# How the reciprocals of the softmax sums reach HBM in turned order: a DMA of single numbers, or a TensorE transpose

## The chip, the cores and the metric

The kernel runs on one core of one Trainium2 chip. The metric is the device time of one execution in microseconds (us); the kernel before took 951.88 us, the median of three runs (951.11 to 956.85). A profile of one execution goes with it. Its engines are PE (TensorE matmuls), PEld (TensorE weight loads), DVE (VectorE), ACT (ScalarE), POOL (GpSimd) and SP (SyncE, which here only issues DMAs). A `q` behind an engine's name means its instruction queue: `SPq` and `ACTq` rows are DMAs being issued.

## What is computed

The reference is one transformer block with adaptive layer norm: 4 batches of 512 tokens with 256 features, 16 attention heads, and a mixture of 16 experts behind the attention. The change touches the attention alone:

```
scores = (einsum('bhqd,bhkd->bhqk', q, k) + einsum('bhqd,bhkd->bhqk', q_rope, k_rope)) * scale
attn = softmax(scores, axis=-1)
out = einsum('bhqk,bhkd->bhqd', attn, v)
out = out.transpose(0, 2, 1, 3).reshape(b, s, H * HD) @ Wout
```

## The kernel before

**Pairs and slots.** The attention goes through 32 head pairs (4 batches of 8 pairs, line 913), numbered `g` from 0 to 31; `LASTP` is 31. A pair has 8 slots: 2 heads by 4 tiles of 128 queries. In a slot, TensorE forms a 128 x 512 tile of scores (`score`, L732) in PSUM. VectorE takes each row's negated maximum (L740), ScalarE computes the exponentials and, in the same instruction, their row sums (L748, into one column of `den[g]`). VectorE transposes the exponentials in blocks of 32 x 32 into `a` (L759). The exponentials are not divided by their sums here; the division comes later, on the small result.

**Turning the blocks.** A full transpose needs the blocks moved between partitions as well. After the last slot, `move(g)` (L768) takes the reciprocals `rd` of the sums (128 queries by 8 numbers, L771) and issues 16 DMAs of 128 KB each from `a` to `et` (L779), 32 rows of 4 KB in each. They are called a train below. `et` has one buffer. `values(g)` (L816) multiplies `et` with the compressed keys and values into `cx` (L823, 16 matmuls), at the start of the pair after the next.

**The division.** `cx` has queries along its free dimension, so its division needs the reciprocals along the free dimension too, repeated on 64 partitions for each head. `everywhere(g)` (L784) does that: TensorE transposes `rd` into a PSUM tile of 8 x 128 (L787), in the `st` ring of four tiles that the scores use as well; one slot later ScalarE copies it to SBUF (L792), and a DMA of 8 rows of 512 bytes writes it to `rdd` in HBM (L793). Two DMAs then read it back, each repeated over 64 partitions, into `rdb` (L795). VectorE multiplies `cx` by `rdb` into `ctxT` (L836), which `project` (L842) multiplies with the output weights.

**Order.** The order on TensorE, VectorE, ScalarE and SP is the order in which the program issues its instructions. The loop at L918 defers each slot's follow-up work to the next slot by the list `then_do`. So, for pair `g`, `move(g)` runs in slot 0 of pair `g+1`; the transpose of `rd` is issued at the end of slot 2 and the copy and the three DMAs follow in slot 3. Pair 31 divides its exponentials at once (L755, L756) and uses no `rdb`. For pair 30 (`LASTP - 1`) half of the train and the write to `rdd` go through ScalarE's queue instead of SP's.

**What else SP issues.** Weights of the experts (L478, L479) in the last batch at slot 4, rows of `xs` for the first expert tiles (L466) in slots 5 and 6 of two pairs, some broadcasts (L162), and register loads before the `xs` rows (L434). ScalarE issues a few: `h2d` (L228) and `tab` (L399), which carry the routing's results to HBM. DMAs of SP and ScalarE take eight completion semaphores (numbers 101 to 108 in the trace) in turn, and a DMA is issued only when the earlier DMA of its semaphore has landed.

After the attention, 79 expert tiles and the shared feed-forward part follow (from L1083), which the change does not touch.

Of the kernel before, what the change touches and what calls it, by code (L numbers as in the profile page):

```python
# [13 lines left out]
F32 = mybir.dt.float32  # L14
# [7 lines left out]
P = 128  # L22
B, S, D = 4, 512, 256
NT = S // P
# [45 lines left out]
def adaln_block(ctx: ExitStack, tc: tile.TileContext, a: dict):  # L70
    nc = tc.nc
# [4 lines left out]
    ident = const.tile([P, P], F32, name="ident")  # L76
# [22 lines left out]
    rdd = dram.tile([B * NPAIR, 2 * NT, P], F32, name="rdd")  # L99
# [3 lines left out]
    psum = ctx.enter_context(tc.tile_pool(name="psum", bufs=2, space=PSUM))  # L103
# [386 lines left out]
    with ExitStack() as actx:  # L490
        aw = actx.enter_context(tc.tile_pool(name="aw", bufs=1))
        big = actx.enter_context(tc.tile_pool(name="big", bufs=2))
        tmp = actx.enter_context(tc.tile_pool(name="tmp", bufs=2))
# [131 lines left out]
        st = {}  # L625
# [111 lines left out]
        def soft(g, slot, pc):  # L737

            nm = tmp.tile([P, 1], F32, tag="nm", name=f"nm_{g}_{slot}", bufs=4)
            nc.vector.tensor_reduce(nm, pc, AX.X, ALU.max, negate=True)  # L740
            if slot == 0:
                den[g] = tmp.tile([P, 2 * NT], F32, tag="den", name=f"den_{g}", bufs=2)
                at[g] = tmp.tile([P, NT, 2, NT, NT, 32], F32, tag="a", name=f"a_{g}")
            if g < LASTP:
                e = tmp.tile([P, S], F32, tag="e", name=f"e_{g}_{slot}", bufs=4)
            else:
                e = at[g].rearrange("p l s h t j -> p (l s h t j)")[:, ts(slot, S)]
            nc.scalar.activation(e, pc, AF.Exp, bias=nm, accum_out=den[g][:, slot : slot + 1])  # L748
            es[g, slot] = e

            def after():
                s, t = divmod(slot, NT)
                if g == LASTP:
                    rd = tmp.tile([P, 1], F32, tag="rd1", name=f"rd_{g}_{slot}", bufs=4)
                    nc.vector.reciprocal(rd, den[g][:, slot : slot + 1])  # L755
                    nc.vector.tensor_scalar(e, e, rd, None, ALU.mult)  # L756
                    return

                nc.vector.transpose(  # L759
                    at[g][:, :, s, :, t, :].rearrange("p l h j -> p h l j"),  # L760
                    e.rearrange("p (h l j) -> p h l j", l=NT, j=32),
                )
                if slot == 2 * NT - 1:
                    move(g)

            return after

        def move(g):  # L768

            rd = tmp.tile([P, 2 * NT], F32, tag="rd", name=f"rd_{g}", bufs=2)  # L770
            nc.vector.reciprocal(rd, den[g])  # L771
            rds[g] = rd

            et[g] = tmp.tile([P, NT, 2, NT, P], F32, tag="et", name=f"et_{g}", bufs=1)

            for q in range(NT):
                for l in range(NT):
                    queue = nc.scalar if g == LASTP - 1 and q >= NT // 2 else nc.sync
                    queue.dma_start(  # L779
                        et[g][ts(l, 32), q].rearrange("p s h n -> p (s h n)"),  # L780
                        at[g][ts(q, 32), l].rearrange("p s h t j -> p (s h t j)"),
                    )

        def everywhere(g):  # L784

            pr = psum.tile([2 * NT, P], F32, tag="st", bufs=4, name=f"prd_{g}")
            nc.tensor.transpose(pr, rds[g], ident)  # L787
            rdT = tmp.tile([2 * NT, P], F32, tag="rdT", name=f"rdT_{g}", bufs=1)
            rdb[g] = tmp.tile([P, S], F32, tag="rdb", name=f"rdb_{g}", bufs=1)

            def after():
                nc.scalar.copy(rdT, pr)  # L792
                (nc.scalar if g == LASTP - 1 else nc.sync).dma_start(rdd[g], rdT)  # L793
                for s in range(2):
                    nc.sync.dma_start(  # L795
                        rdb[g][ts(s, 64), :],
                        rdd[g, ts(s, NT), :].rearrange("t p -> (t p)").unsqueeze(0).to_broadcast([64, S]),
                    )

            return after  # L800

# [112 lines left out]
        LASTP = len(pairs) - 1  # L914
        den, at, es, et, rds, rdb = {}, {}, {}, {}, {}, {}
        then_do = []
        ahead = None
        for g, (b, j) in enumerate(pairs):  # L918
            then = pairs[g + 1] if g < LASTP else None
            for slot in range(2 * NT):  # L920
# [28 lines left out]
                if slot == 2 and g:  # L949
                    then_do.append(everywhere(g - 1))  # L950
# [132 lines left out]
    turned, chosen, g, yts = {}, {}, {}, {}  # L1083
# [131 lines left out]
```

## Time and profile before

| | |
|---|---|
| median of three runs | 951.88 us |
| the profiled execution | 950.73 us |
| its span, first to last instruction | 948.5 us |
| mean granted TensorE clock | 0.98 |
| the 32 head pairs, scores to last ctxT | about 33 to 653 us of the span |
| transposes of rd (L787) | 31 of 0.27 us |
| copies of the transposed rd (L792) | 31 of 0.24 us |
| writes of rdd issued (L793) | 30 by SP, 1 by ScalarE, median 0.42 us to issue |
| et DMAs issued (L779) | 488 by SP, median 0.59 us; 8 by ScalarE |
| DMA packets | 79,361, 140.64 MB |

A row of the timeline has the start in us from the span's start, the duration in us, engine, line, operation, the tiles written and read, and, where instructions in a row were merged, their count; a bracket tells for how long the engine stood idle before it and what ended that. A row of the waits has who waited, for what, the time in total, the number of times and the longest, in us. The stretches view gives, for each stretch of time, its length and the busy time of each engine with its number of instructions.

### The profile page before, as it was taken

The page shows a single profiled execution, that of the slowest core. Times are in us where ns is not written, and L with a number is a line of the kernel's source. Part 1 is how long each engine was busy: PE and PEld are TensorE (multiplying, and loading weights), DVE is VectorE, ACT ScalarE, POOL GpSimd, SP SyncE. Part 2 cuts the span into 40 slices and gives each one's busy share as a digit, 9 for nine tenths or more (in the row PEclk, how much of TensorE's full clock was granted, in tenths as well). Part 3 has the DMA queues.
Part 4 walks back from the last instruction along what each step waited for, and adds up shares of the span by engine and source line. Part 5 has one row for each costly group of instructions (what it writes and reads, how often), then busy time and mean ns, then how long its engine had stood idle before and what let it go on. Part 6 is the DMA issues. An engine that isn't in the chain of part 4 may idle for free. (4 is left out here: it accounts for less than half of the span.)

```text
span 948.5 us, 12482 instructions
## 1 busy us (share of the span) xinstructions
PE 884.5 (93%) x3199; PEld 476.6 (50%) x3199; DVE 630.2 (66%) x1377; ACT 429.3 (45%) x1030; POOL 451.9 (48%) x412
## 2 busy tenths in 40 slices
PE   5888999999999999998999998959899999999996
PEld 3323444444444444453444454425666677777754
DVE  1488688788879888879988889844353332232258
ACT  2344545464644654554455554423533434444410
POOL 3644355355634776843377864313624623433421
PEclk9899999999999999999999999979989999999999
DMA  9526466575456665555477776675553443333274
GB/s 253 184 68 145 113 143 151 125 161 127 100 134 156 164 176 142 128 132 139 107 182 181 210 178 171 173 195 182 182 139 90 136 133 96 112 119 95 66 282 161
DMA packets 79361, 140.64 MB, mean 148 GB/s; under 512 B 22873, under 2 KB 47160, under 8 KB 79292
## 3 DMA queue, kind: packets, MB, share of 16 engines
q1 hardware_dynamic: 71352, 119.84, 50.6%
q0 software_dynamic: 6864, 16.86, 4.9%
q10 hardware_dynamic: 1076, 3.15, 1.0%
q8 instruction: 27, 0.44, 0.2%
q14 instruction: 42, 0.34, 0.1%
HBM read 51.35 MB, written 25.39 MB: 81 GB/s over the span
## 5 line engine op out<-in xcount | busy, mean ns | idle before, releaser
L732 PE MATMUL psc<-w 128*128 128x512 f32 x512 | 264.2, 609 | 22.9 <-ACT a L748 11.5
L748 ACT ACTIVATE e<-psc,nm 128x512 f32<-128x512 f32 x248 | 170.3, 687 | 219.6 <-DVE nm L740 218.6
L740 DVE TENSOR_REDUCE nm<-psc 128x1 f32<-128x512 f32 x256 | 171.5, 670 | 68.0 <-PE psc L732 67.6
L711 POOL TENSOR_TENSOR w<-w 128x512 f32<-128x512 f32 x64 | 81.6, 1276 | 199.0 <-ACT w L708 196.9
L759 DVE STREAM_TRANSPOSE a<-e 128x512 f32<-128x512 f32 x248 | 172.0, 694 | 0.1
L1022 POOL DMA_INDIRECT ys<-y,xt x79 | 77.2, 977 | 138.4 <-ACT y L1021 125.7
L732 PEld LDWEIGHTS psc<-w 128*128 128x128 f32 x512 | 92.1, 192 | 95.1 <-issue 66.6
L823 PE MATMUL cx<-et,ckv 128*64 128x512 f32 x512 | 117.8, 602 | 3.5 <-DVE rows L183 1.2
L996 PE MATMUL ph<-w,xT 128*128 x316 | 108.7, 467 | 1.0 <-DVE xT L990 0.7
L714 POOL TENSOR_TENSOR w<-w 64x512 f32<-64x512 f32 x64 | 82.1, 1283 | 37.8 <-DVE w L713 34.0
L1002 DVE TENSOR_TENSOR g<-g,ph 128x176 f32<-128x176 f32 x79 | 26.7, 338 | 93.8 <-ACT g L1001 93.8
L1017 PE MATMUL py<-w,gT 88*128 x316 | 83.0, 385 | 3.2 <-ACT gT L1010 3.2
L715 POOL TENSOR_TENSOR w<-w 64x512 f32<-64x512 f32 x64 | 80.9, 1264 | 4.7
L858 PEld LDWEIGHTS po<-wvo,ctxT 128*128 128x128 f32 x256 | 48.4, 192 | 61.3 <-issue 59.0
L858 PE MATMUL po<-wvo,ctxT 128*128 128x256 f32 x256 | 76.7, 384 | 0.8 <-DVE ctxT L834 0.8
L823 PEld LDWEIGHTS cx<-et,ckv 128*64 128x64 f32 x512 | 35.1, 137 | 82.4 <-issue 59.2
L1017 PEld LDWEIGHTS py<-w,gT 88*128 88x128 f32 x316 | 60.5, 192 | 25.2 <-ACT gT L1010 5.2
L197 POOL DMA_INDIRECT xs<-rows,si x48 | 47.7, 994 | 42.0 <-ACT a L748 24.1
L996 PEld LDWEIGHTS ph<-w,xT 128*128 128x128 f32 x316 | 54.9, 194 | 18.9 <-issue 1.0
L705 PE MATMUL ppk<-w 128*128 128x512 f32 x128 | 63.0, 615 | 0.0
L705 PE MATMUL ppq<-w 128*128 128x512 f32 x128 | 61.0, 599 | 1.4 <-DVE ctxT L836 1.4
L1021 ACT ACTIVATE y<-py,xt 128x256 f32<-128x256 f32 x79 | 37.4, 473 | 46.0 <-PE py L1017 46.0
(201 smaller groups left out, 1107.1 us busy)
## 6 DMA issues: line engine op xcount, KB each, us to landing
et<-a SPq DMA_DIRECT2D x488, 128.0 KB
xt<-xs SPq DMA_DIRECT2D x79, 129.0 KB
w<-ys SPq DMA_DIRECT2D x16, 512.0 KB
rdb<-rdd SPq DMA_DIRECT2D x62, 128.0 KB
w<-in_we SPq DMA_DIRECT2D x16, 352.0 KB
w<-in_wl SPq DMA_DIRECT2D x16, 176.0 KB
xs<-fill SPq DMA_DIRECT2D x17, 129.0 KB
x<-in_x SPq DMA_DIRECT2D x4, 512.0 KB
```

The lines of the kernel that those rows point to most:

```text
L705: nc.tensor.matmul(pp, w_j[:, j, ts(k, P)], d["hT"][:, k, :], start=(k == 0), stop=(k == KD - 1))
L711: nc.gpsimd.tensor_tensor(t1, t0[which], rope[:, 0, :], ALU.mult)
L714: nc.gpsimd.tensor_tensor(dst[64:128, 0, :], t1[64:128, :], t3[which][64:128, :], ALU.add)
L715: nc.gpsimd.tensor_tensor(dst[0:64, 1, :], t1[0:64, :], t3[which][0:64, :], ALU.add)
L732: nc.tensor.matmul(pc, st[b]["qb"][j][:, s, ts(t, P)], kb[j % 2][:, s, :], start=True, stop=True)
L740: nc.vector.tensor_reduce(nm, pc, AX.X, ALU.max, negate=True)
L748: nc.scalar.activation(e, pc, AF.Exp, bias=nm, accum_out=den[g][:, slot : slot + 1])
L759: nc.vector.transpose(at[g][:, :, s, :, t, :].rearrange("p l h j -> p h l j"), e.rearrange("p (h l j) -> p h l j", l=NT, j=32),)
L823: nc.tensor.matmul(cx[s * 64 : s * 64 + 64, :].rearrange("p (q n) -> p q n", q=NT), d["ckv"][:, k, 0, :], et[g][:, :, s, k, :], start=(k = ...
L858: nc.tensor.matmul(d["po"][t2][:, t % 2, :], d["ctxT"][j][:, ts(t, P)], wvo[:, j, :], start=False, stop=(j == NPAIR - 1 and t % 2 == 1),)
L996: nc.tensor.matmul(ph, xT[:, k, :], we[:, k * 2 * I : (k + 1) * 2 * I], start=(k == 0), stop=(k == KD - 1),)
L1017: nc.tensor.matmul(py, gT[:, f, :], we[0:I2, WE + f * D : WE + (f + 1) * D], start=(f == 0), stop=(f == 1))
```

## The change

For pairs 0 to 29 the reciprocals are written to HBM straight from `rd`: one DMA on SP, issued in `move(g)` ahead of the train, with `rdd[g]` viewed as 128 x 8, so that each of the 1,024 numbers of 4 bytes goes to its own place. The transpose, its PSUM tile, ScalarE's copy and the DMA behind it are gone for these pairs. The two DMAs that read `rdd` back stay in slot 3. Pair 30 keeps the old way.

```
         def move(g):
             rd = tmp.tile([P, 2 * NT], F32, tag="rd", name=f"rd_{g}", bufs=2)
             nc.vector.reciprocal(rd, den[g])
             rds[g] = rd
+            if g < LASTP - 1:
+
+                nc.sync.dma_start(rdd[g].rearrange("t p -> p t"), rd)
...
         def everywhere(g):

-            pr = psum.tile([2 * NT, P], F32, tag="st", bufs=4, name=f"prd_{g}")
-            nc.tensor.transpose(pr, rds[g], ident)
-            rdT = tmp.tile([2 * NT, P], F32, tag="rdT", name=f"rdT_{g}", bufs=1)
             rdb[g] = tmp.tile([P, S], F32, tag="rdb", name=f"rdb_{g}", bufs=1)

-            def after():
-                nc.scalar.copy(rdT, pr)
-                (nc.scalar if g == LASTP - 1 else nc.sync).dma_start(rdd[g], rdT)
+            def spread_out():
                 for s in range(2):
                     nc.sync.dma_start(
                         rdb[g][ts(s, 64), :],
                         rdd[g, ts(s, NT), :].rearrange("t p -> (t p)").unsqueeze(0).to_broadcast([64, S]),
                     )
+
+            if g < LASTP - 1:
+                return spread_out
+            pr = psum.tile([2 * NT, P], F32, tag="st", bufs=4, name=f"prd_{g}")
+            nc.tensor.transpose(pr, rds[g], ident)
+            rdT = tmp.tile([2 * NT, P], F32, tag="rdT", name=f"rdT_{g}", bufs=1)
+
+            def after():
+                nc.scalar.copy(rdT, pr)
+                nc.scalar.dma_start(rdd[g], rdT)
+                spread_out()

             return after
```

## The prediction

> **What bounds the kernel now.** I read the page's busy shares first, then single head pairs in the stretches view, then TensorE's and SP's timelines, then SP's waits.
>
> ```profile
> PE 884.5 (93%) x3199; PEld 476.6 (50%) x3199; DVE 630.2 (66%) x1377; ACT 429.3 (45%) x1030; POOL 451.9 (48%) x412
> ```
>
> One head pair, from one start of the cx matmuls to the next (PE, PEld, DVE, ACT and POOL busy, then clock, DMA share and GB/s):
>
> ```profile
> 166.57:183.35 16.78, 16.78 (x52) 7.45 (x51) 13.09 (x25) 8.59 (x23) 8.73 (x8) 1.00 0.61 141
> 183.35:200.13 16.78, 16.78 (x52) 7.45 (x52) 14.04 (x32) 7.94 (x21) 8.58 (x7) 1.00 0.61 141
> ```
>
> TensorE is busy for all of the 16.78 us, at full clock, and VectorE has some 3 us left. TensorE sets the pace of such pairs. The transpose that goes stands in it so:
>
> ```profile
> 322.34 0.27 PE L787 MATMUL prd<-ident,rd 128*8 128x128 f32 x1
> 322.45 1.02 PE L732 MATMUL psc<-w 128*128 128x512 f32 x2
> ```
>
> It lasts 0.27 us, but the next matmul starts 0.11 us after it: ends are modelled and matmuls overlap, so 0.11 is what it takes of the pace.
>
> The second loop is the train of 16 DMAs that turns et:
>
> ```profile
> 318.05 10.06 SPq L779 DMA_DIRECT2D et<-a  x16
> 328.20 0.42 SPq L793 DMA_DIRECT2D rdd<-rdT  x1
> 330.31 1.12 SPq L795 DMA_DIRECT2D rdb<-rdd  x2
> ```
>
> et has one buffer: a train starts when the cx matmuls of the pair before have ended, takes SP 10.06 us to issue, and its data is read by the next cx matmuls at 331.14. From the timelines I took, for each of the 30 trains that the change touches, two margins. *Cover* is the time from the reciprocal's end to the train's start: mean 1.9 us, and none in trains 0, 12, 20, 22 and 25. *Slack* is the time from the landing (last packet plus 0.6 us, the gap where TensorE does wait) to the cx matmuls: mean 1.8 us, none in trains 0, 11, 13, 19 and 29. So TensorE waits for et in five trains and is close to it in others. SP's waits say the same of the cover:
>
> ```profile
> SPq L779 <- PE cx L823: 54.7, 24, 4.5
> SPq L795 <- DMA rdd<-rdT: 50.6, 31, 3.4
> ```
>
> **Removed.** *TensorE:* 30 transposes x 0.11 us = 3.3 us. Where TensorE waits for et (five trains) the time is given back at the wait, so 25 x 0.11 = **-2.7**; nothing if something else fills the pace. *ScalarE:* 30 copies x 0.24 us, nothing: ScalarE is 45% busy and waits for VectorE's maxima. *PSUM:* one of four st buffers is free for some 3 us more in each pair; TensorE's waits for an st buffer all stand seven or more score matmuls behind the transpose, where it is no longer among the last four tiles, so nothing. *SP's wait* of 50.6 us for rdd: rdb can follow the train at once, some 2.0 us sooner, because the numbers went out 10 us before. rdb's reader is a pair away, so that itself brings 0 (at most the 2.2 us that VectorE now waits for rdb). But what is queued behind rdb on SP moves too: expert weights and xt loads in the last batch. One place has them on the path:
>
> ```profile
> 616.66 0.54 SPq L478 DMA_DIRECT2D w<-in_we  x1
> ...
> 621.28 11.30 SPq L779 DMA_DIRECT2D et<-a  x8
> ```
>
> ```profile
> 619.09 12.57 ACTq L779 DMA_DIRECT2D et<-a  x8
> 631.70 0.69 ACT L748 ACTIVATE a<-psc,nm 128x512 f32<-128x512 f32 x1 [12.57 <-DMA et<-a]
> ```
>
> SP and ScalarE take the same eight DMA semaphores in turn, and a DMA waits until the earlier one of its semaphore has landed. Here the last train waits for weight loads so, ScalarE stands for 12.57 us, and TensorE for 11.55. Weights issued 1.9 us earlier (end of rdb at 616.56 against 614.65) should land that much earlier: **-1.9** (0 if transfers, not issues, set it).
>
> **Added.** A DMA of 128 x 8 single numbers on SP, ahead of the 16 et DMAs, waiting for the reciprocal. All 16 are queued behind it, and the cx matmuls wait for them. *Issue:* the row with as many pieces (128 x 8, of 512 bytes) is
>
> ```profile
> 3.80 1.38 SPq L534 DMA_DIRECT2D w<-in_wqr  x2
> ```
>
> 0.67 us each. The upper end is the value loads, also 1,024 pieces but behind full queues: 4.37 us for two, 2.2 each. I take 0.67, since the queues are nearly empty when it is issued (DMA share 0.09 from 330 to 332 us). *Transfer:* the nearest row writes 17 single numbers to HBM through one DMA engine; first its issue on ScalarE's queue, then the DMA queues in the 0.2 us after it (packets, MB, share of 16 engines; one packet is the semaphore's):
>
> ```profile
> 463.34 0.48 ACTq L399 DMA_DIRECT2D tab<-ei  x1
> ```
>
> ```profile
> q10 hardware_dynamic: 18, 0.00, 4.9%
> ```
>
> Its packets are 6 ns apart (464.06 to 464.17), and SP, which waits for it, goes on at 464.59. The new DMA has 64 numbers on each of 16 engines: 64 x 6 ns = 0.4 us, landing some 1.8 us after its issue. The Trainium skill speaks against this: "DMA: Bandwidth & Descriptors", Specifications, says that below 512 bytes the engine reads, modifies and writes, and its section "Latency and other measured facts" gives 0.2 us for an HBM access. One after another, 64 x 0.2 = 12.8 us an engine (estimate from that page). The row contradicts that for 17 numbers: they would take 3.4 us, and all took 1.25. I take the row. But another row makes me keep a wide upper end: the third tab, 46 numbers on two engines, has its last packet at 709.51 and is recorded as landed at 713.94, and packets of xt beside it took up to 3.7 us where 47 ns is usual. That is (713.94 - 709.51)/46 = 96 ns a number; nothing in the trace tells why this one was slow.
>
> Let X be the time by which the numbers hold up a train that has no cover. A train loses max(0, X - cover - slack), and the sum over the 30 trains is: X 0.75: 0.8 us (train 0 alone); 2.0: 4.8; 3.0: 13.5; 5.0: 49; 6.0: 73; 12.8: 273. A pair that is held up gives the next train more cover, so the loss is between half of that sum and all of it. With issue 0.67 + 0.05 and the transfer beside the train's spare DMA time (share 0.91), X = 0.75: **+0.8**. At 2.2 us of issue it is about +6.
>
> *Semaphores in turn:* each pair still issues 19 DMAs, but one of them moves ahead of the train. Five trains (11, 19, 21, 27, 29) stop because ScalarE's h2d or tab DMA has the semaphore that a late et DMA needs, for example
>
> ```profile
> SPq L779 <- DMA tab<-ei: 2.0, 1, 2.0
> ```
>
> If the stop comes one et DMA earlier, one more has to be issued behind it: 5 x 0.63 us, less 0.2 of slack = +3.0; if the stops fall away, the waits of trains 11, 19 and 29 go (1.2 + 0.5 + 0.4): -2.0. The order can't be read from the trace; I take **+1.5**, half of the case in which the stop moves.
>
> POOL's queue and ScalarE's order are not passed by anything that moves; rd has two buffers, so the reciprocal that would wait for the new DMA to read is two pairs away.
>
> **Sum.** -2.7 - 1.9 + 0.8 + 1.5 = -2.3 us. The profiled execution took 950.73 us (span 948.5 and 2.2 around it), so 948.4; the median of the runs is 1.15 above it: 951.88 - 2.3 = **949.6**. About 1% (9.5 us) is what a measurement of this kernel can tell from no change.
>
> **Rivals.**
>
> *A, likeliest, 53%: within 1%.* As summed. With TensorE's gain lost, the issue at 2.2 us and the semaphores at +3.0 it ends near 958; with all ends good, near 944. Its own range is 944 to 958.
>
> *B, 32%: slower, the small writes are slow to drain.* Place: the et trains. At 96 ns each, spread over the engines, 64 x 0.096 = 6.1 us; less the 1.0 us that a train's own first packet needs anyway and what spare DMA time regains, X is about 5.2: 27 to 54 us, say 40, which gives some 990. It decides from X of 2.9 to 3.7 us on, where the loss passes 11.8 us. For it: the third tab, and 16 numbers going to each 64-byte stretch of rdd. Against it: two of the three tabs. Also for it in part: the new DMA's semaphore is the one that the eighth et DMA takes, 4.5 us into the train.
>
> *C, 11%: the writes go through one place in HBM, one after another.* At 12.8 us of X: 1,090 to 1,220; at 1,024 x 96 ns = 98 us, half of 30 x (98 - 3.7), or more: over 2,300. Against it: scatters of 1,032-byte rows, whose ends are partial too, land in 2.4 us at best, as most scatters of whole rows do.
>
> *D, 4%: faster.* The turn of semaphores happens to spare the last train its waits: of TensorE's 11.55 us some 8 more go, 941.
>
> The range that leaves out C and most of D, with B up to X of about 6: 944 to 1003. Faster by over 1%: 0.04; within: 0.53; slower: 0.43.
>
> **What would show it.** The new DMA's row with 0.7 us (2.2 would be the upper end); its start at the reciprocal's end, and trains still starting as the cx matmuls end; trains still of 10.06 us (longer, with a stop at the eighth DMA, is B); no wait of SP for rdd; TensorE's wait near 620 us at 9 to 10 us. Pairs of 16.67 us confirm the 0.11. The forecast is wrong if TensorE waits for et in most pairs, or if the last train's stop changes by several us.

## The result, and the profile after

The changed kernel takes 996.84 us, the median of five runs (993.69 to 1004.91); the kernel before took 953.44 us beside it (951.11 to 958.32). The recorded ratio is 1.0483, with a 95% interval of 1.0438 to 1.0528: slower by 4.8%. (The quotient of the two medians, 1.0455, lies inside that interval.) The profiled execution took 1004.91 us, the longest of the five, with a span of 1002.7, 54.2 us more than the span before. 50.8 of these lie in the attention (the first ctxT of pair 30 starts at 694.58 us instead of 643.74), 3.4 behind it.

On the page after, the packets are 30,719 more than before, nearly all of them the 30 x 1,024 numbers; the bytes are the same. What the engines wait for has changed:

```profile
PE 898.9 (90%) x3169; PEld 481.6 (48%) x3169; DVE 630.3 (63%) x1377; ACT 425.2 (42%) x1000; POOL 453.6 (45%) x412
...
DMA packets 110080, 140.63 MB, mean 140 GB/s; under 512 B 53833, under 2 KB 77880, under 8 KB 110012
...
L832 PE MATMUL cx<-et,ckv 128*64 128x512 f32 x512 | 125.4, 633 | 27.8 <-DMA et<-a 18.6
...
L714 POOL TENSOR_TENSOR w<-w 64x512 f32<-64x512 f32 x64 | 82.4, 1287 | 67.1 <-DMA xs<-rows,si 29.8
```

TensorE has 30 matmuls fewer and is busy for 14.4 us longer. The cx matmuls, in front of which TensorE stood idle for 3.5 us in all before, now wait 27.8. GpSimd waits 29.8 us for its own row scatters (`xs`), for which it did not wait at this line before. The same two groups before, and two of TensorE's waits:

```profile
L823 PE MATMUL cx<-et,ckv 128*64 128x512 f32 x512 | 117.8, 602 | 3.5 <-DVE rows L183 1.2
L714 POOL TENSOR_TENSOR w<-w 64x512 f32<-64x512 f32 x64 | 82.1, 1283 | 37.8 <-DVE w L713 34.0
```

```profile
PE psc L732 <- ACT a L748: 11.5, 1, 11.5
...
PE psc L732 <- POOL w L714: 4.3, 2, 2.8
```

SP's and TensorE's waits after:

```profile
SPq L782 <- DMA rdd<-rd: 64.3, 21, 6.0
SPq L782 <- PE cx L832: 58.7, 22, 5.7
SPq L775 <- DVE rd L771: 42.8, 16, 6.0
...
SPq L782 <- DMA et<-a: 8.8, 10, 3.4
```

```profile
PE psc L732 <- POOL w L714: 23.5, 10, 6.2
PE cx L832 <- DMA et<-a: 18.6, 7, 5.1
...
PE psc L732 <- ACT a L748: 7.9, 1, 7.9
```

The first line of SP's is the new one: in the middle of 21 trains SP stands, three microseconds a time, until the numbers have landed. SP's old wait for the write of rdd at the rdb DMAs (50.6 us) is down to one of 3.8, for pair 30. SP's timeline around train 6:

```profile
175.48 1.18 SPq L793 DMA_DIRECT2D rdb<-rdd  x2
178.16 0.37 SPq L775 DMA_DIRECT2D rdd<-rd  x1
181.09 11.32 SPq L782 DMA_DIRECT2D et<-a  x16
```

The DMA of the numbers is issued in 0.37 us. The view of the DMA queues from 179.0 to 179.8 us holds just that transfer (queue, packets, MB, share of 16 engines):

```profile
q1 hardware_dynamic: 1040, 0.00, 58.3%
```

So all 1,024 numbers, and 16 packets of the semaphore, have passed the DMA engines 1.6 us after the issue. But the semaphore shows the transfer complete only at 186.68 us, 8.5 us after the issue. In between little else moves; the next view is from 179.8 to 186.6 us, a row of DMA share in 40 slices (0.17 us each) above the packets:

```profile
DMA  0000000000000099948994949399909508000248
...
DMA packets 218, 0.63 MB, mean 93 GB/s; under 512 B 64, under 2 KB 64, under 8 KB 218
```

The first et DMAs were issued from 181.09 us on and carry 4 KB packets; 154 packets of that size start in these 6.8 us, where one et DMA alone has 32, and seven of them were issued. The first lands at 186.85, 5.8 us after its issue (2.4 is usual, the median in the trace before and in the experiments without a hold-up), the next six from 187.14 to 189.00, 0.25 to 0.55 us apart. The eighth et DMA has the semaphore of the numbers and is issued at 186.70, as soon as they have landed. Over the 30 pairs the numbers land 8.23 to 12.26 us after their issue, 9.54 in the median. (Landing times here and below are from the start of a DMA's issue to its last semaphore event in the trace.)

### The profile page after: what moved, and what is told of

Same layout as the page of the kernel before. It is cut to its first block, busy times and chain, and to the rows that moved or that the text cites. A ratio compares the mean times of both kernels' runs of the same rounds, so it can differ in the third digit from the quotient of the medians.

```text
span 1002.7 us, 12366 instructions
## 1 busy us (share of the span) xinstructions
PE 898.9 (90%) x3169; PEld 481.6 (48%) x3169; DVE 630.3 (63%) x1377; ACT 425.2 (42%) x1000; POOL 453.6 (45%) x412
## 2 busy tenths in 40 slices
DMA packets 110080, 140.63 MB, mean 140 GB/s; under 512 B 53833, under 2 KB 77880, under 8 KB 110012
## 5 line engine op out<-in xcount | busy, mean ns | idle before, releaser
L732 PE MATMUL psc<-w 128*128 128x512 f32 x512 | 269.6, 620 | 37.5 <-POOL w L714 23.5
L732 PEld LDWEIGHTS psc<-w 128*128 128x128 f32 x512 | 94.8, 194 | 117.5 <-issue 65.7
L832 PE MATMUL cx<-et,ckv 128*64 128x512 f32 x512 | 125.4, 633 | 27.8 <-DMA et<-a 18.6
L714 POOL TENSOR_TENSOR w<-w 64x512 f32<-64x512 f32 x64 | 82.4, 1287 | 67.1 <-DMA xs<-rows,si 29.8
L832 PEld LDWEIGHTS cx<-et,ckv 128*64 128x64 f32 x512 | 39.5, 145 | 113.1 <-issue 86.8
L708 ACT COPY w<-ppk 128x512 f32<-128x512 f32 x32 | 18.7, 585 | 94.5 <-PE ppk L705 94.5
```

What stands on the lines that cost most here:

```text
L714: nc.gpsimd.tensor_tensor(dst[64:128, 0, :], t1[64:128, :], t3[which][64:128, :], ALU.add)
L732: nc.tensor.matmul(pc, st[b]["qb"][j][:, s, ts(t, P)], kb[j % 2][:, s, :], start=True, stop=True)
L832: nc.tensor.matmul(cx[s * 64 : s * 64 + 64, :].rearrange("p (q n) -> p q n", q=NT), d["ckv"][:, k, 0, :], et[g][:, :, s, k, :], start=(k = ...
```

## Experiments

All ratios are against the kernel before, run on the same chip. The three chips used had medians for it of 946.85 (kernels 1 to 4), 951.25 (5, 6, 7 and 11) and 952.60 us (8, 9, 10 and 12). Where there is no interval, the kernel was run once. A pair is named here by its train: pair 14 is the time from the cx matmuls of pair 13 to those of pair 14, in which the numbers and the train of pair 14 go out.

**1. Rows of 32 bytes in place of single numbers.** Is it the place in front of the train, or the pieces?

```
-                nc.sync.dma_start(rdd[g].rearrange("t p -> p t"), rd)
+                nc.sync.dma_start(rdd[g].rearrange("t (q n) -> (t q) n", n=2 * NT), rd)
```

> As the changed kernel, but the reciprocals go out unturned: 128 rows of 32 bytes instead of 1,024 single numbers, so the division uses them in the wrong order. Theory 1 (the single writes drain slowly, about 7 us for 1,024, and the eighth et DMA, which takes the semaphore of the number DMA, waits for it): the DMA lands in about 2 us, no train is stopped, and the time is what the forecast's likeliest case gave, 0.995 to 1.000 of before. Theory 2 (the drain blocks the DMA engines, whatever the semaphores do): the same here. Rival (it is the place in front of the train, an early write to HBM or the early read back that costs, not the number of pieces): the time stays near the changed kernel, 1.03 to 1.05 of before.

943.61 us, ratio 0.9964 (0.9950 to 0.9979). The DMA lands 1.40 us after its issue in the median, most trains take some 10.1 us again, and TensorE's waits are much those of before:

```profile
PE psc L732 <- ACT a L748: 9.8, 1, 9.8
PE pt L638 <- ACT xn_a L149: 9.5, 1, 9.5
PE psc L732 <- ACT e L748: 6.7, 8, 2.3
PE psc L732 <- POOL w L714: 4.6, 2, 2.8
```

Everything in the change but the single numbers is therefore worth -0.36%, 3.4 us (2.0 to 4.7 by the interval). The forecast's sum, -2.3 us or -0.24%, is the forecast for this kernel.

**2. Half of the numbers.** Does the drain go by the count?

```
-                nc.sync.dma_start(rdd[g].rearrange("t p -> p t"), rd)
+                nc.sync.dma_start(rdd[g, 0:NT].rearrange("t p -> p t"), rd[:, 0:NT])
...
-                        rdd[g, ts(s, NT), :].rearrange("t p -> (t p)").unsqueeze(0).to_broadcast([64, S]),
+                        rdd[g, ts(s if g >= LASTP - 1 else 0, NT), :].rearrange("t p -> (t p)").unsqueeze(0).to_broadcast([64, S]),
```

> As the changed kernel, but only the first head's 512 numbers are written, and the second head is divided by the first head's sums. If the drain goes by the number (7 us for 1,024), it lands after some 5 us instead of 8.4; the eighth et DMA comes 4.5 us into the train, so trains with 0.5 us of cover and more are not stopped any longer: 0.998 to 1.008 of before. If it is a fixed delay of such a DMA, landing stays at 8 us and the time at 1.04 to 1.05.

989.73 us, ratio 1.0426 (1.0391 to 1.0461). 512 numbers land in 7.06 to 10.55 us, median 8.42, against 9.54 for 1,024. SP's waits hardly shrink:

```profile
SPq L782 <- DMA rdd<-rd: 50.1, 18, 4.9
...
SPq L782 <- DMA et<-a: 10.4, 11, 2.1
```

A fixed price for each number on its DMA engine, which rival B had assumed (64 x 0.096 us), would have taken some 3 us off. It is not that.

**3. Single numbers only in the 22 pairs without scatters.** In pairs 14 to 17 and 23 to 26 GpSimd sends its row scatters; there the turn is made as before. The edit replaces `g < LASTP - 1` by membership in this list, and gives the eight pairs' write of `rdT` back to SP:

```
+QUIET = [g for g in range(NPAIR * B - 2) if g not in (14, 15, 16, 17, 23, 24, 25, 26)]
...
-            if g < LASTP - 1:
+            if g in QUIET:
```

> Numbers written by SP only in the 22 pairs beside which GpSimd scatters no rows (all of 0 to 29 but 14 to 17 and 23 to 26); those eight keep the transpose. Comparing the two traces pair by pair, some 27 of the 51 us that the attention grew lie in the eight pairs, where GpSimd's rope additions wait for scatters that landed 7 to 12 us late. So 1.020 to 1.030 of before if the two parts add; under 1.010 if the scatters are all of it; 1.045 if they are not part of it.

972.67 us, ratio 1.0247 (1.0213 to 1.0281). The scatters land in 2.4 to 6.4 us again, and GpSimd's wait for them is no longer among its waits. TensorE's largest:

```profile
PE cx L833 <- DMA et<-a: 18.0, 10, 5.1
PE pt L639 <- ACT xn_a L150: 9.6, 1, 9.6
PE psc L733 <- ACT a L749: 8.0, 1, 8.0
```

(Its line numbers are one higher.) The eight pairs with scatters are thus about half of the loss, 0.0483 - 0.0247 = 2.4%, and the late trains of the others the rest. The trace of the changed kernel gives the same split: against before, pairs 14 to 17 and 23 to 26 grew by 12.9 and 15.0 us, all others together by 23.0.

**4. The same 22 pairs, the numbers issued by GpSimd.** Their DMA then has a semaphore of its own, outside the eight that SP and ScalarE take in turn. The edit to kernel 3 is `nc.gpsimd` for `nc.sync`.

> As the one with the 22 quiet pairs, but GpSimd issues the number DMA; GpSimd's DMAs have semaphores of their own, so no et DMA shares its semaphore. Theory 1: trains go back to 10.1 to 10.6 us and the time to 0.995 to 1.005 of before, unless making 1,024 descriptors takes GpSimd so long that its rope additions become late (then 1.01 and more, with GpSimd named in the waits for the scores). Theory 2: trains are still issued in 10 us but et lands late, and the time stays with the run in which SP issues for the same pairs.

977.13 us, ratio 1.0334 (1.0284 to 1.0384). The numbers land in 8.89 us in the median. SP no longer waits for them, but:

```profile
SPq L783 <- DMA et<-a: 65.2, 33, 7.5
```

The trains still stop: the et DMAs in front land late behind the numbers, so that it is their semaphores which are late when they come round again. The stop does not depend on whose semaphore the numbers have. Part of this kernel's time is its own fault (GpSimd waited 60.3 us for reciprocals, and TensorE stood once for 13.8 us in front of cx), so its ratio says nothing finer.

**5. A 64-byte stretch of HBM for each number.** With the count out, the next suspect was that 16 numbers share 64 bytes of `rdd`.

```
+    fars = dram.tile([B * NPAIR, P, 2 * NT, 16], F32, name="fars")
+    far = [fars[i, :, :, 0] for i in range(B * NPAIR)]
...
-                nc.sync.dma_start(rdd[g].rearrange("t p -> p t"), rd)
+                nc.sync.dma_start(far[g], rd)
...
-                        rdd[g, ts(s, NT), :].rearrange("t p -> (t p)").unsqueeze(0).to_broadcast([64, S]),
+                        (rdd[g, ts(s, NT), :].rearrange("t p -> (t p)") if g >= LASTP - 1 else a["tri"][0:NT, :].rearrange("t p -> (t p)")).unsqueeze(0).to_broadcast([64, S]),
```

> Each of the 1,024 numbers of a pair goes to a 64-byte stretch of HBM of its own (the same 1,024 single pieces, the same place in the order of issue); the numbers read back are taken from another table of the kernel, so the reciprocals are left out of the output. After two runs in which half the numbers took nearly as long as all (8.42 against 9.54 us), three theories are left. The line theory (the pieces that land in one 64-byte line follow one another, as 16 numbers[...] share each line of the turned table): with a line each they land in about 2 us, and the time is that of the rows of 32 bytes, 0.994 to 0.999. The number theory (each single number costs a DMA engine some 0.1 us wherever it goes): they land as late as before, 8 to 10 us, and the ratio is 1.04 to 1.05. The reach theory (scattered addresses over 64 KB are slower still): over 10 us, ratio above 1.05.

949.46 us, ratio 0.9980 (0.9960 to 1.0000). They land in 3.65 us in the median, and SP's train of that time is whole:

```profile
168.52 0.59 SPq L777 DMA_DIRECT2D fars<-rd  x1
171.75 10.24 SPq L784 DMA_DIRECT2D et<-a  x16
```

The line theory said about 2 us and the time of kernel 1: the time came, the landing is 1.7 us later than it said. That single numbers as such cost the 4.8% is out: the page counts the same 110,080 packets as for the changed kernel. (`rdb` reads another table here, so this kernel also has no wait between the two; kernel 1 shows that wait to be nothing.)

**6. Single numbers, not turned.** The same pieces, but the eight numbers of a partition one behind the other, as in kernel 1:

```
-            rd = tmp.tile([P, 2 * NT], F32, tag="rd", name=f"rd_{g}", bufs=2)
+            rd2 = tmp.tile([P, 2 * NT, 2], F32, tag="rd", name=f"rd_{g}", bufs=2)
+            rd = rd2[:, :, 0]
...
-                nc.sync.dma_start(rdd[g].rearrange("t p -> p t"), rd)
+                nc.sync.dma_start(rdd[g].rearrange("t (q n) -> (t q) n", n=2 * NT), rd)
```

> The same 1,024 single pieces, but unturned: the eight numbers of a partition lie behind one another in HBM, and the source is a tile with every second number used, so that the pieces stay single. (The order of the numbers in HBM is not turned, so each column of the context is scaled with another column's reciprocal.) A 64-byte line is then written by two neighbouring partitions[...]. If what is slow is several engines writing to one line, the numbers land in 2 to 3 us and the ratio is 0.994 to 1.005. If what is slow is any single number that follows another into the same line, whoever writes it, they land as late as before, 7 to 10 us, ratio 1.035 to 1.05. If it is the count of single numbers on an engine, the same 7 to 10 us; the run with a line for each number tells these two apart.

998.95 us, ratio 1.0522 (1.0468 to 1.0576); landing 6.69 to 12.38 us, median 8.55. So turning is not to blame either: the same 4 KB of HBM written as 128 rows takes 1.40 us, and written as 1,024 numbers 8.55, in the same order of addresses. (No view tells which DMA engine carries which number, so whether several engines write to one line was not tested.)

**7. The numbers of 88 partitions.** `rd[0:88, :]` into the first 88 columns, with `rdb` reading as in kernel 5.

> Only the numbers of the first 88 partitions are sent, 704 in place of 1,024, in turned order (numbers read back are taken from another table, so the reciprocals are left out of the output). If the drain goes by the numbers of one engine (64 on each of eleven engines), it stays at 9 to 10 us, and et DMAs of the five engines without numbers land in time but their DMA as a whole does not. If it goes by what HBM takes in all, some 9.5 x 704/1,024 = 6.6 us. If by the numbers in a 64-byte line, 9 to 10 us again, since 88 partitions fill the same lines of which 11/16 are written. Ratio 1.03 to 1.05 in the first and last, 1.015 to 1.03 in the second.

967.10 us (one run; 1.017 of the median before). Landing 5.82 to 10.24 us, median 6.87: as the second theory said, which was that HBM takes so many numbers in a time. But kernel 2 with fewer numbers (512) took longer, 8.42. Both put 16 numbers to a 64-byte stretch (in kernel 7 but for the last stretch of a row), and by the count alone 512 should have landed before 704. How a partial set of partitions or of rows shortens the drain stays open.

**8, 9, 10. Fewer to a stretch.** Turned order with numbers 8 and 16 bytes apart (in 64 bytes 8 and 4), and the unturned order with each partition's eight numbers alone in 512 bytes; `rdb` reads as in kernel 5. The edits to the destination are

```
+    fars = dram.tile([B * NPAIR, 2 * NT, P, 2], F32, name="fars")
+    far = [fars[i, :, :, 0].rearrange("t p -> p t") for i in range(B * NPAIR)]
```

with a 4 in place of the 2 for the second, and `fars[g][:, 0 : 2 * NT]` of a [P, 128] tile with the source of kernel 6 for the third.

> With a 64-byte stretch for each number they landed in 3.65 us, with 16 to a stretch in 9.54 (turned) and 8.55 (unturned). Here the numbers lie 8 bytes apart in turned order: 8 to a 64-byte line, 64 to 512 bytes (numbers read back come from another table, so the reciprocals are left out of the output). If numbers of one line follow one another, each after the first takes (9.54 - 3.65) / 15 = 0.39 us, and they land in 3.65 + 7 x 0.39 = 6.4 us. If it is numbers of one 512-byte block (128 to a block, with 8 to a block at 64 bytes apart: 5.89 / 120 = 0.049 us each), they land in 3.65 + 56 x 0.049 = 6.4 us too: this run gives the size, the run with eight numbers alone in 512 bytes tells the two apart. If only 4-byte pieces that touch are slow, about 3.7 us.

> As before with the numbers 16 bytes apart: 4 to a 64-byte line, 32 to 512 bytes (reciprocals left out of the output). By line 3.65 + 3 x 0.39 = 4.8 us to landing, by block 3.65 + 24 x 0.049 = 4.8 us; about 3.7 us if only pieces that touch are slow; the same as with 8 to a line if what counts is that a line is shared at all. Time within 2% of the kernel before.

> The eight numbers of a partition behind one another as single pieces (the source has every second number), each partition's eight alone in 512 bytes of HBM: 8 to a line, 8 to 512 bytes (reciprocals left out of the output). If the 64-byte line is what they queue for: as with 8 to a line in turned order, 6 to 7 us. If the 512-byte block is: as with 64 bytes apart, 3.2 to 4 us. If what counts is that one DMA engine writes the next number of a line while the last is under way: longer than the turned order with 8 to a line, in which an engine's next piece lies in another line.

One run each: 950.27, 947.71 and 967.86 us, with 952.60 before. Together with the others, from the 30 DMAs of each trace:

| pieces of a pair | in 64 bytes | landing, us: least, median, most | ratio |
|---|---|---|---|
| 128 rows of 32 bytes (1) | 2 rows | 1.38, 1.40, 3.55 | 0.9964 |
| 1,024 numbers, 16 bytes apart (9) | 4 | 2.71, 3.11, 6.41 | 0.995, one run |
| 1,024 numbers, 64 bytes apart (5) | 1 | 3.19, 3.65, 6.32 | 0.9980 |
| 1,024 numbers, 8 bytes apart (8) | 8 | 4.13, 4.52, 6.67 | 0.998, one run |
| 1,024 numbers, eight together in 512 bytes (10) | 8 | 5.75, 6.51, 10.52 | 1.016, one run |
| 704 numbers, close, turned (7) | 16 | 5.82, 6.87, 10.24 | 1.017, one run |
| 512 numbers, close, turned (2) | 16 | 7.06, 8.42, 10.55 | 1.0426 |
| 1,024 numbers, close, unturned (6) | 16 | 6.69, 8.55, 12.38 | 1.0522 |
| 1,024 numbers, close, turned (the change) | 16 | 8.23, 9.54, 12.26 | 1.0483 |

At the same 1,024 packets of 4 bytes, the landing goes from 3.1 to 9.5 us with how close the destinations lie. The 512-byte block is out as what they queue for: eight numbers alone in 512 bytes land at 6.51 us, where the block theory said 3.2 to 4. Stretches of 32 or of 64 bytes are left. In 32 bytes lie 1, 2, 4, 8, 8 and 8 numbers in runs 5, 9, 8, 10, 6 and in the change; that order fits as well as by 64, and no run here separates them. A third reading is open too, that pieces are slow where they touch: in runs 5, 8 and 9 no two numbers touch, and they land in 3.1 to 4.5 us; in runs 2, 6, 7, 10 and in the change they do, and they land in 6.5 to 9.5. Only that run 8 took 4.52 us, where this reading said 3.7, speaks against it. A fixed price for each further number (0.39 us by 64 bytes) fails: it said 6.4 and 4.8 us for runs 8 and 9, which took 4.52 and 3.11; the dear part is the step from 8 to 16 in 64 bytes (or from 4 to 8 in 32, or to pieces that touch). The right column also shows between which landings it begins to cost: one of 4.5 us is hidden, one of 6.5 is not.

**11. VectorE makes the turn.** A kernel with the reference's computation and without single numbers: the reciprocals go into a tile of 128 x 32, VectorE turns it by blocks of 32 x 32, and one DMA writes 128 rows of 128 bytes to the places of the turned order in a table of its own, from which `rdb` is read.

```
+            nc.vector.reciprocal(rd if g == LASTP - 1 else wide[:, 0 : 2 * NT], den[g])
...
+                rdw = tmp.tile([P, 32], F32, tag="rdT", name=f"rdw_{g}", bufs=1)
+                nc.vector.transpose(rdw, wide)
+                nc.sync.dma_start(rdw_d[g].rearrange("t (q j) -> q t j", j=32), rdw)
```

> The turn made by VectorE: the reciprocals go into a tile of 128 x 32, VectorE turns it in blocks of 32 x 32, and one DMA writes its 128 rows of 128 bytes to HBM in turned order; neither TensorE nor ScalarE has a part in it, and no single numbers are written. What TensorE gains (25 x 0.11 us = 2.7) and the earlier issue of expert weights stay as with the rows of 32 bytes (0.9964); VectorE pays some 0.1 to 0.3 us a pair, and a train may start that much later. If pieces of a row are what matters, the numbers land in 1.4 to 2 us and the ratio is 0.994 to 0.999. If rows of 128 bytes are still held up, landing 3 us or more, the ratio is 1.00 to 1.02.

952.24 us, ratio 1.0012 (0.9988 to 1.0036). The numbers land in 1.98 us in the median, and VectorE pays 0.21 us a pair:

```profile
L779 DVE STREAM_TRANSPOSE rdw<-wide 128x32 f32<-128x32 f32 x30 | 6.3, 212 | 1.0
```

The loss is gone; a gain does not show.

**12. The same, its DMA behind the train.**

```
-                nc.sync.dma_start(rdw_d[g].rearrange("t (q j) -> q t j", j=32), rdw)
...
+            if g < LASTP - 1:
+                nc.sync.dma_start(rdw_d[g].rearrange("t (q j) -> q t j", j=32), rdw)
```

> VectorE's turn as before (0.9988 to 1.0036), but the DMA of the numbers is issued behind the 16 et DMAs and not in front of them. In front of them it held the train of pair 0 up (+0.7 us) and took the turn of a semaphore; behind them it has until the rdb DMAs, some us later. If the place in front costs what the forecast said (0.8 + 1.5 us), the time falls by some 2 us against that version: 0.996 to 1.000. If VectorE's second operation is what ate the gain, it stays at 1.000 to 1.003. If the rdb DMAs now wait for the numbers and the context's last product for those, above 1.003.

951.40 us, ratio 0.9983 (0.9966 to 1.0001). The ratio is 0.0029 below kernel 11's, some 2.8 us where some 2 were expected, but the two ratios come from different chips, their intervals overlap, and this one reaches 1. SP again waits for the write at each pair, and no engine waits for `rdb`:

```profile
SPq L800 <- DMA rdw_d<-rdw: 44.8, 30, 2.3
```

## Why the prediction was wrong

The time was forecast at 949.6 us with 53%, and at 990 with 32%, for slow small writes; it came to 996.84, inside the range of 944 to 1003.

**The step that failed** is "The new DMA has 64 numbers on each of 16 engines: 64 x 6 ns = 0.4 us, landing some 1.8 us after its issue". The 0.4 us is right for the packets (1,040 in under 0.8 us). But packets passing is not landing: the landing took 9.54 us in the median. The row chosen as the nearest, 17 numbers on one engine in 1.25 us, had too few numbers to show it, and the row that was nearer, the third tab's 46 numbers with 4.4 us from the last packet to landing, was kept for the upper end. The Trainium skill's rule in "DMA: Bandwidth & Descriptors", Specifications (below 512 bytes the engine reads, modifies and writes) was set aside. The 12.8 us that I had estimated from the page for an engine's numbers, one after another, is too much, and the rule says nothing of closeness, on which 3.1 to 9.5 us depend here. A read and a write that must follow one another in one stretch could explain why close numbers are slow, but no view here shows reads of HBM for these packets, and numbers 16 bytes apart landed sooner (3.11 us) than numbers 64 bytes apart (3.65). Why closeness costs stays open. The observation "16 numbers going to each 64-byte stretch of rdd" stood in rival B as one point among others; that the numbers lie so close is what decided.

**X.** Forecast at 0.75, rival B at 5.2. The five trains that had no cover before (0, 12, 20, 22 and 25) now take SP 13.0 to 15.9 us to issue instead of 10.1 to 10.5, 3.0 to 5.6 us more. B's X had the right size. B's sum for X = 5.0 was 49 us or half of it; the pairs outside the scatters grew by 23.0 net of gains. Train 0, which loses first, gives the next trains cover (9.09 us for train 1), as the prediction said of pairs held up.

**What B lacked** is the other half. GpSimd's scatters stand behind the numbers too, as kernel 3 confirms: in pairs 14 to 17 and 23 to 26, 24 of the 32 land in 7.0 to 12.4 us and the other eight in 2.3 to 5.0, where before it was 2.4 to 5.7 for all. GpSimd waits for its scatters before its next rope addition, the scores wait for that, and TensorE stands. Its timeline in pair 14, and TensorE's:

```profile
337.55 1.27 POOL L711 TENSOR_TENSOR w<-w 128x512 f32<-128x512 f32 x1 [0.99 <-ACT w L708]
346.71 1.27 POOL L714 TENSOR_TENSOR w<-w 64x512 f32<-64x512 f32 x1 [7.89 <-DMA xs<-rows,si]
```

```profile
352.46 3.78 PE L732 MATMUL psc<-w 128*128 128x512 f32 x4 [6.22 <-POOL w L714]
```

"POOL's queue and ScalarE's order are not passed by anything that moves" was true of the queues of instructions and wrong for the engines that carry their transfers. That B ended near the right time with half of its causes is partly luck.

**Removed, -2.7 us for the transposes.** Confirmed where nothing waits: the stretch from one start of the cx matmuls to the next, pair 13 and then pair 14 after (length, busy PE, PEld, DVE, ACT, POOL, clock, DMA share, GB/s):

```profile
314.56:331.22 16.66, 16.66 (x50) 7.61 (x50) 12.55 (x23) 6.70 (x16) 8.74 (x8) 1.00 0.76 175
331.22:356.17 24.95, 18.73 (x51) 7.85 (x50) 16.36 (x34) 12.16 (x29) 14.02 (x14) 0.88 0.78 119
```

16.66 is the predicted 16.67. In kernel 1, 15 of the 30 stretches are shorter than before by 0.07 to 0.11 us; the sum of -2.7 was not measured apart.

**Weights earlier, -1.9 us.** TensorE's wait near 620 us was 11.5; it is 9.8 in kernel 1 (-1.7) and 7.9 in the changed kernel (-3.6), against the 9 to 10 that the prediction named.

**Issue, 0.67 us.** 0.37 was measured: dearer rows were taken than needed, without consequence.

**Semaphores, +1.5 us.** The stops that this term is about stayed nearly as they were: with the DMA in the same place, kernel 1's SP waits for `h2d` and `tab` in front of et DMAs for 9.8 + 4.0 us, against 10.1 + 4.7 before. So the +1.5 did not come. In all, kernel 1 came out 3.4 us below before, where the sum was 2.3, which lies inside its interval. That the eighth et DMA takes the semaphore of the numbers came true, but kernel 4 shows that the stop comes without it.

## What to carry to other kernels

Ask of a DMA not only how long its packets take, but when it lands, and what else the same DMA engines have to carry behind it: here, behind 4 KB of numbers, a 128 KB DMA of SP landed in 5.8 us instead of 2.4, and scatters of GpSimd in up to 12.4. Single numbers written close together are the bad case; rows of 32 bytes to the same 4 KB landed in 1.4 us, so turn the data on an engine before it goes out. (VectorE's block transpose cost 0.21 us a pair; that kernel was no faster than the one before.) Numbers that are spaced out landed in 3.1 to 4.5 us, but the runs with them did not read them back. Before a row of the profile is taken as the price of something larger, look for the row with the most pieces, even if it is the odd one.

## What the runs showed that was not expected

TensorE's waits cost more than their length. In pair 14 the pair grew by 8.17 us: 6.22 of waiting, and 1.95 of more busy time for the same work, because the granted clock fell. Stretches of the changed kernel behind waits of TensorE of 5.07, 2.75, 2.25, 2.89 and 2.10 us, and then the one of 6.22, with the clock as the third number from the right:

```profile
79.80:85.50 5.70, 5.70 (x17) 1.71 (x17) 0.69 (x1) 0.00 (x0) 0.00 (x0) 0.63 0.17 28
...
158.56:164.00 5.44, 5.44 (x17) 1.90 (x18) 0.70 (x2) 0.00 (x0) 0.00 (x0) 0.69 0.46 98
232.25:236.00 3.75, 3.75 (x17) 1.40 (x18) 0.60 (x1) 0.41 (x2) 0.00 (x0) 1.00 0.26 42
...
314.56:320.00 5.44, 5.44 (x21) 2.14 (x22) 2.59 (x5) 0.78 (x2) 0.00 (x0) 1.00 0.56 134
373.73:379.00 5.27, 5.27 (x12) 1.69 (x14) 3.83 (x8) 3.45 (x9) 4.44 (x5) 0.68 0.59 137
```

```profile
352.40:360.00 7.60, 7.54 (x20) 2.33 (x20) 3.06 (x7) 1.56 (x4) 5.84 (x7) 0.69 0.72 81
```

After the two longest waits the clock is 0.63 and 0.69 over the next 6 to 8 us. The shorter ones do not go by their length: after 2.10 and 2.75 us it is 0.68 and 0.69, after 2.25 and 2.89 it is full. The Trainium skill, "TensorE: Matmul & The Clock Gate", Part 1, has the array at half clock after an idle window of about 3.4 us and until as long a busy one; here waits of 2.10 and 2.75 us were enough, and what else decides stays open. From pair 0's cx matmuls to pair 30's ctxT, the changed kernel and then kernel 1, with the same matmuls:

```profile
79.80:694.58 614.78, 554.85 (x1726) 251.22 (x1727) 461.67 (x954) 281.67 (x662) 301.29 (x263) 0.97 0.76 141
77.08:640.45 563.37, 538.68 (x1726) 246.05 (x1727) 461.28 (x958) 281.98 (x666) 300.67 (x263) 0.99 0.64 154
```

TensorE was busy for 554.9 us against 538.7: by this some 16 of the 51 us are the lower clock. No rival had a term for it.
